# Graph network on one core: gathers that add into SBUF instead of identity matmuls, and ScalarE's and TensorE's parts of VectorE's chains issued one step later

## The chip, the core and the metric

The kernel runs on one core of a Trainium2 chip. A core has five engines with an instruction queue each, served in order: TensorE (PE, with its weight loads PEld), VectorE (DVE), ScalarE (ACT), GpSimd (POOL) and SyncE (SP). SP, ACT and POOL also issue DMAs. The metric is device microseconds (us) of one execution, from the first to the last instruction with what lies around it.

## The reference

There are 6250 nodes with 64 features and 200,000 directed edges, sorted by destination. Two graph layers follow one another, each with a residual and a layer norm around it.

```python
def layer0(v, src, dst):                       # gated attention, one head
    z = v @ Wa
    e = leaky_relu(concat([pre_w * z[src], z[dst]]) @ att_w)
    alpha = segment_softmax(e, dst)
    h = segment_sum(alpha * z[src], dst)
    pw = pre_w * v[src]
    max_feat, mean_feat = segment_max(pw @ Wg, dst), segment_mean(pw, dst)
    return sigmoid(concat([v, max_feat, mean_feat]) @ gate_w) * h

def layer1(x, edges, src, dst):                # 3 layers, 8 heads of 8
    edge_attr = relu(ln(edges) @ eW1 + eb1) @ eW2 + eb2
    for l in range(3):
        h = ln(x)
        q = h[dst] @ Wq
        k = h[src] @ Wkn + edge_attr @ Wke
        val = h[src] @ Wvn + edge_attr @ Wve
        alpha = segment_softmax((q * k).sum(-1) / sqrt(8), dst)
        agg = segment_sum(val * alpha, dst)
        gate = sigmoid(agg @ Wih + h @ Whh)
        x = x + (agg + gate * (h @ Wself - agg)) @ Wout
        x = x + relu(ln(x) @ mW1 + mb1) @ mW2 + mb2
    return ln(x)
x = ln(x + layer0(x)); x = ln(x + layer1(x))   # biases left out above
```

What matters here is the sum in `k` and `val`: a node row, looked up by the edge's source, plus a term made from the edge's own features. A table row of 128 floats holds a node's `h @ Wkn` and `h @ Wvn` side by side.

## The kernel before

**Tiling.** The nodes are sorted by degree and cut into 49 blocks (NB) of 128, one node per partition. A block's edges lie in slots along the free dimension: slot k of all 128 nodes is one column. `ORDER` runs block 1, block 48 (LB, which has 106 real nodes), block 0, then the others by falling degree.

**Edge stage** (L573 to L1004). 52 iterations (`NB + 3`), each with up to four blocks at different ages: `bs[0]` gets its lists and `masks`; `bs[1]` normalises its edge features (`even`) and sorts its slots (`select`); `bs[2]` does layer 0's attention (`absorb`) and begins the edge network; `bs[3]` ends it (`features`, half 1). `select` gives 16 of a node's slots (NW) to windows, which are later looked up by TensorE with one-hot matrices, and the rest (`LCAPS`, 14 to 40 per block, 1142 in all) to gathers.

The order is written out by hand. Each iteration has 8 steps. VectorE's work is in Python generators, which yield the cost of the piece just issued; at each step the loop takes pieces from the job that is furthest behind its weight (25 for `absorb`, 26 for the chain of `even`, `masks` and `select`) until the step's share is done (L981). A piece issues its ScalarE and TensorE instructions where they stand, such as `f_sq` (L697), `s_tg` (L752), the exponential (L896), the tanh (L934), and in `prepare` the transpose (L548), ScalarE's `fht`, the table's matmul (L559) and the copies of `p_kv` (L562, L563, L567), between which VectorE makes `p_rest` and the last part of `p_kv` (L566, L569). Around the pieces stand `aim` (VectorE's `f_mv`, L812), `order` (TensorE's `f_tr`, L825, and ScalarE's `f_xt`), and the edge network (L862, L865, L844, L848). SP issues the stores of `xd`, `x1`, `ht` and of the one-hot matrices `oh_d` (L792), and the loads `f_xs` (L805). POOL gathers layer 0's rows (L679) and stores finished table rows of a block (`place_rows`, L537).

**Three layers** (L1034 to L1282). At a layer's start ScalarE issues seven loads of the table's bf16 parts (`ftb`, L1040). Then 53 iterations take a block each. For a block, `todo` lists one window part of 16 slots and one to three gathered parts of up to 20 slots (CL). `gather` takes the next part of the whole layer as soon as one of four buffers `g1` comes free, and issues one indirect DMA per slot: 128 rows of 512 bytes from the table (L1067). `sums` adds up to 8 slots in a PSUM tile `b_pk`: TensorE first writes the edge terms (L1089), then adds for a window part the one-hot products (L1101), or for a gathered part the gathered rows by a matmul with the identity:

```python
if g is not None:
    nc.tensor.matmul(pk[:, h, :c, :], ident, g[:, u0 - k0 + h : u0 - k0 + n : 2, :], start=False, stop=True)
    continue
```

ScalarE copies the sums to `b_k` and `b_v` (L1105, L1108). VectorE multiplies with the queries (`scores`, L1112, L1113), and one iteration later makes the softmax (`soft`) and the weighted sum (`values`, L1130, L1131). The steps `turned`, `gate`, `update`, `updated`, `turned2`, `hidden`, `close` and `prepare` turn that into the node's new row, over the block's next three iterations, between the next blocks' groups of sums. SP loads edge terms (`eal`, L1051), one-hot matrices (`ohl`, L1057) and node tiles (L1073, L1075). At the end of an iteration POOL stores finished table rows for the next layer (L537), or in the last layer the output (L1221). A layer's first gather waits for all table stores of the one before.

Of the kernel before, what the change touches and what calls it, by code (L numbers as in the profile page):

```python
# [16 lines left out]
P = 128  # L17
D = 64
H = 8
# [54 lines left out]
CL = 20  # L74
# [347 lines left out]
def passes(ctx, tc, ins, out, meta_d, t0_d, own_d, ident, row_f, ones, norm_c, st_i, id_i, off, end, has, hash_, rdeg,  # L422
# [118 lines left out]
    def prepare(wk, mps, w, b, xb, i):  # L541

        tab, hd = tabs[i], ht_d[i]
        hn = wk.tile([P, D], F32, name="p_hn")
        norm(wk, hn, xb)
        yield
        pt = mps.tile([D, P], F32, name="p_pm")
        nc.tensor.transpose(pt, hn, ident)  # L548
        ht = hts[turn[0] % 3]
        turn[0] += 1  # L550
        nc.scalar.activation(ht[:D, :], pt, AF.Identity, bias=w["nrm"][:, 1:2], scale=w["nrm"][:, 0:1])

        n = P if b < LB else LN
        nc.sync.dma_start(hd[b][:, :n], ht[:, :n])
        if b == 0:
            nc.sync.dma_start(hd[LB][:, LN:P], ht[:, :SPARE])
        yield
        pm = mps.tile([P, W1], F32, name="p_pm")
        nc.tensor.matmul(pm, ht, w["wc"][:, D : 3 * D], start=True, stop=True)  # L559
        kv = wk.tile([P, WT], F32, name="p_kv", bufs=3)  # L560
        part = kv[:, W1:].bitcast(BF).rearrange("p (k d) -> p k d", k=3)
        nc.scalar.copy(kv[:, :W1], pm)  # L562
        nc.scalar.copy(part[:, 0], kv[:, :W1])  # L563
        yield
        rest = wk.tile([P, W1], F32, name="p_rest")
        nc.vector.tensor_tensor(rest, kv[:, :W1], part[:, 0], ALU.subtract)  # L566
        nc.scalar.copy(part[:, 1], rest)  # L567
        yield
# [5 lines left out]
    with tc.tile_pool(name="e1", bufs=1) as wp, tc.tile_pool(name="e_g", bufs=4) as gp, \  # L574
# [51 lines left out]
        def meet(b):  # L626
# [5 lines left out]
            ow = mp.tile([P, FO], F32, name="ow")  # L632
# [51 lines left out]
        def even(b):  # L684
# [8 lines left out]
            sqs = []  # L693
            for k0 in range(0, c, 12):
                k1 = min(k0 + 12, c)
                sq = wk.tile([P, 12, D], F32, name="f_sq")
                nc.scalar.activation(sq[:, : k1 - k0], xe[:, k0:k1], AF.Square)  # L697
                sqs.append((k0, k1, sq))
                if len(sqs) == 2:
                    yield 2.0  # L700
                    for k0, k1, sq in sqs:
                        nc.vector.tensor_reduce(sm[:, 1, k0:k1], sq[:, : k1 - k0], AX.X, ALU.add)
                    sqs = []
            if sqs:
                yield 1.5
            for k0, k1, sq in sqs:
                nc.vector.tensor_reduce(sm[:, 1, k0:k1], sq[:, : k1 - k0], AX.X, ALU.add)
# [6 lines left out]
            yield 4.5  # L714

        def select(b):
# [35 lines left out]
            nc.scalar.copy(tg[:, :c], v)  # L752
            yield 1.6

            pt = mps.tile([P, 4 * P], F32, name="p_pm")
            for h in range(2):
                nc.tensor.matmul(pt[h * D : (h + 1) * D, :D], tg, ident[:, slice(h, P, 2)], start=True, stop=True)
            m["tt"] = tt = wk.tile([P, D], F32, name="s_tt")
            nc.scalar.copy(tt, pt[:, :D])
# [21 lines left out]
            for w0 in range(0, NW, 4):  # L781
# [4 lines left out]
                bc = wk.tile([P, 4, P], F16, name="s_bc")  # L786
                nc.scalar.copy(bc, pb)
                yield 0.2
# [84 lines left out]
        def absorb(b):  # L873
# [18 lines left out]
            acc = wk.tile([P, 2 * D + 3], F32, name="a_acc")  # L892
# [3 lines left out]
            nc.scalar.activation(ex, e, AF.Exp, bias=o3[:, 0:1], accum_out=o3[:, 1:2])  # L896
            nc.vector.scalar_tensor_tensor(sc[:, 1, :], sc[:, 1, :], 1.0, vm, op0=ALU.mult, op1=ALU.mult,
                                           accum_out=o3[:, 2:3])
            yield 1.4
            for i, (k0, k1, g) in enumerate(m["g"]):  # L900
# [6 lines left out]
            for i, o, op in ((0, mx, ALU.max), (1, h, ALU.add)):  # L907
                if n == 1:
                    nc.vector.tensor_copy(o, part[:, 0, i, :])
                for j in range(1, n):  # L910
                    nc.vector.tensor_tensor(o, part[:, 0, i, :] if j == 1 else o, part[:, j, i, :], op)
            o4 = wk.tile([P, 5], F32, name="a_o4")
# [21 lines left out]
            nc.scalar.activation(o4[:, 2:3], o4[:, 2:3], AF.Tanh, bias=ow[:, D + 1 : D + 2], scale=0.5)  # L934
# [10 lines left out]
            for _ in prepare(wk, mps, nxt, b, xb, 0):  # L945
                yield 1.5
# [1028 lines left out]
```

## Time and profile before

| what | value |
|---|---|
| median of the 3 runs | 8554.21 us (8543.06 to 8555.53) |
| profiled execution | 8539.47 us |
| its span, first to last instruction | 8537.4 us |
| mean granted TensorE clock | 0.789 |
| busy in the span | PE 6224.1, PEld 4258.2, DVE 6013.9, ACT 2476.6, POOL 5161.1 us |
| before the edge stage | 0 to 110 us |
| edge stage | 110 to 3625 us |
| layers 0, 1, 2, each from its first gather | from 3625, 5261 and 6899 us; the last ends at 8537 us |
| DMA, read from and written to HBM | 899.50 and 236.89 MB |

A row of the groups gives line, engine, operation, output and inputs by the program's names, shapes and count; then busy time and mean ns of one; then the engine's idle time just before these and what ended most of it. A row of the waits gives who waited for whom, total us, times and the longest. A row of the timeline gives start, duration, engine, line, operation and, in brackets, the idle time before and its releaser; "issue" means that the trace shows nothing that was waited for. A row of the DMA queues gives packets, MB and the share of the time of 16 DMA engines.

### The profile page before, as it was taken

The page shows a single profiled execution, that of the slowest core. Times are in us where ns is not written, and L with a number is a line of the kernel's source. Part 1 is how long each engine was busy: PE and PEld are TensorE (multiplying, and loading weights), DVE is VectorE, ACT ScalarE, POOL GpSimd, SP SyncE. Part 2 cuts the span into 40 slices and gives each one's busy share as a digit, 9 for nine tenths or more (in the row PEclk, how much of TensorE's full clock was granted, in tenths as well). Part 3 has the DMA queues.
Part 4 walks back from the last instruction along what each step waited for, and adds up shares of the span by engine and source line. Part 5 has one row for each costly group of instructions (what it writes and reads, how often), then busy time and mean ns, then how long its engine had stood idle before and what let it go on. Part 6 is the DMA issues. An engine that isn't in the chain of part 4 may idle for free. (4 is left out here: it accounts for less than half of the span.)

```text
span 8537.4 us, 150270 instructions
## 1 busy us (share of the span) xinstructions
PE 6224.1 (73%) x58044; PEld 4258.2 (50%) x58044; DVE 6013.9 (70%) x13393; ACT 2476.6 (29%) x5234; POOL 5161.1 (60%) x5439
## 2 busy tenths in 40 slices
PE   3555556666656666768888886888888868888976
PEld 2222222333333333356666664666666656667765
DVE  6867778778777777647677664666676656777866
ACT  1333333333333333412222221222222212222221
POOL 4555545555444444277777773777777557777772
PEclk6767777777677676788888887888888878888887
DMA  5445444445444444366566664555566555556653
GB/s 120 130 113 131 120 118 130 127 130 134 116 117 112 112 119 124 90 171 157 145 157 155 154 150 118 147 142 149 154 155 153 134 138 134 144 146 151 159 138 77
DMA packets 965722, 1146.65 MB, mean 134 GB/s; under 512 B 665161, under 2 KB 713110, under 8 KB 957962
## 3 DMA queue, kind: packets, MB, share of 16 engines
q1 hardware_dynamic: 504569, 642.88, 24.1%
q0 software_dynamic: 180144, 412.30, 24.0%
q10 hardware_dynamic: 280288, 81.76, 4.4%
q8 instruction: 465, 7.62, 0.4%
q14 instruction: 256, 2.09, 0.1%
HBM read 899.50 MB, written 236.89 MB: 133 GB/s over the span
## 5 line engine op out<-in xcount | busy, mean ns | idle before, releaser
L1067 POOL DMA_INDIRECT g<-tab,fidx x3426 | 3275.1, 956 | 1103.5 <-issue 1009.0
L679 POOL DMA_INDIRECT g<-ft_d,si x1596 | 1527.7, 957 | 1625.1 <-DVE wx L663 1026.5
L1101 PE MATMUL b_pk<-ftb,ohl 128*128 128x128 bf16 x21609 | 1375.8, 229 | 19.4 <-DMA ftb<-tab 19.4
L1101 PEld LDWEIGHTS <-ohl 128*128 128x128 bf16 x21609 | 1325.0, 104 | 65.5 <-issue 41.4
L1112 DVE TENSOR_TENSOR b_k<-b_k,b_qe 128x1024 f32<-128x1024 f32 (+11 forms) x402 | 446.3, 1110 | 1102.9 <-ACT b_k L1105 870.3
L1093 PE MATMUL b_pk<-g,fident 128*128 128x384 f32 (+3 forms) x2172 | 1028.8, 601 | 219.9 <-DMA g<-tab,fidx 180.5
L844 PE MATMUL f_pe<-f_hid,fw 128*64 128x448 f32 (+3 forms) x2320 | 710.7, 700 | 595.1 <-ACT ea L848 594.9
L1105 ACT COPY b_k<-b_pk 128x512 f32<-128x512 f32 (+2 forms) x753 | 404.7, 537 | 2257.9 <-PE b_pk L1101 1252.3
L1089 PE MATMUL b_pk<-fwkv,eal 64*128 64x128 f32 x11556 | 1037.8, 317 | 0.0
L825 PE MATMUL f_tr<-f_mv,f_xs 128*64 128x40 f32 (+11 forms) x12544 | 603.0, 269 | 510.5 <-ACT f_xt L829 291.9
L825 PEld LDWEIGHTS f_tr<-f_mv,f_xs 128*64 128x64 f32 x12544 | 571.2, 183 | 740.3 <-issue 348.1
L1089 PEld LDWEIGHTS b_pk<-fwkv,eal 64*128 64x128 f32 x11556 | 860.2, 215 | 100.8 <-issue 27.8
L862 PE MATMUL f_ph<-f_xt,fw 64*128 64x448 f32 (+3 forms) x2320 | 723.1, 723 | 38.1 <-ACT f_xt L829 35.0
L1093 PEld LDWEIGHTS b_pk<-g,fident 128*128 128x128 f32 x2172 | 420.4, 216 | 517.1 <-issue 317.6
L1131 DVE TENSOR_REDUCE b_ag<-b_v 128x64 f32<-128x2624 f32 (+18 forms) x147 | 660.9, 4496 | 5.1
L844 PEld LDWEIGHTS f_pe<-f_hid,fw 128*64 128x64 f32 x2320 | 143.2, 168 | 1013.3 <-ACT ea L848 760.5
L865 ACT ACTIVATE f_hid<-f_ph,fb 128x896 f32<-128x896 f32 (+3 forms) x580 | 557.0, 976 | 268.9 <-PE f_ph L862 197.1
L1113 DVE TENSOR_REDUCE b_al<-b_k 128x128 f32<-128x1024 f32 (+11 forms) x402 | 446.7, 1111 | 13.8
L1105 ACT COPY b_v<-b_pk 128x512 f32<-128x512 f32 (+2 forms) x753 | 410.4, 545 | 0.0
L1130 DVE TENSOR_TENSOR b_v<-b_v,b_qe 128x2624 f32<-128x2624 f32 (+18 forms) x147 | 406.0, 2762 | 0.0
L862 PEld LDWEIGHTS f_ph<-f_xt,fw 64*128 64x128 f32 x2320 | 235.1, 238 | 292.9 <-ACT f_xt L829 147.5
L812 DVE TENSOR_TENSOR f_mv<-s_tt,e_fac 128x608 f32<-128x608 f32 (+11 forms) x392 | 313.9, 810 | 90.7 <-PE f_tr L825 52.8
(360 smaller groups left out, 7721.0 us busy)
## 6 DMA issues: line engine op xcount, KB each, us to landing
ohl<-oh_d SPq DMA_DIRECT2D x588, 384.0 KB
eal<-ea_d SPq DMA_DIRECT2D x174, 512.0 KB
oh_d<-s_oh SPq DMA_DIRECT2D x196, 384.0 KB
g<-tab,fidx POOLq DMA_INDIRECT x3426
eal<-ea_d SPq DMA_DIRECT2D x93, 384.0 KB
eal<-ea_d SPq DMA_DIRECT2D x66, 448.0 KB
ea_d<-ea ACTq DMA_DIRECT2D x130, 224.0 KB
g<-ft_d,si POOLq DMA_INDIRECT x1596
```

The costliest lines, as they stand in the source:

```text
L679: nc.gpsimd.indirect_dma_start(out=g[:, k - k0, :], out_offset=None, in_=t0_d[:], in_offset=bass.IndirectOffsetOnAxis(ap=got[b]["si"][:, k ...
L825: nc.tensor.matmul(pv[r * D : (r + 1) * D, j], xss[(4 * ORDER.index(b) + 4 * j0 // D) % 4][:, (j0 + j) % (D // 4), :], mv[:, j, :, r::2], ...
L844: nc.tensor.matmul(pe[h * D : (h + 1) * D, :w], w2[:, s, :], hid[s][:, h, :w], start=(s == 0), stop=(s == 1))
L862: nc.tensor.matmul(ph[:, h, :w], w1[r, s * P : (s + 1) * P], xf[r, e0 * D : e1 * D], start=True, stop=True)
L865: nc.scalar.activation(hid[s][:, :, :w], ph[:, :, :w], AF.Relu, bias=b1[:, s : s + 1])
L1067: nc.gpsimd.indirect_dma_start(out=g[:, k - k0, :], out_offset=None, in_=tab.rearrange("n (k d) -> (n k) d", d=D), in_offset=bass.Indirect ...
L1089: nc.tensor.matmul(pk[:, j % 2, j // 2, :], ea[r, e, :], w["wkv"][r], start=(j < 2), stop=False)
L1093: nc.tensor.matmul(pk[:, h, :c, :], ident, g[:, u0 - k0 + h : u0 - k0 + n : 2, :], start=False, stop=True)
L1101: nc.tensor.matmul(pk[:, h, j, :], o, tbh[:, cl + NW * u, i, :], start=False, stop=(j == c - 1 and u == us[-1] and i == 2))
L1105: nc.scalar.copy(to.rearrange("p (j h) d -> p h j d", h=2), pk[:, :, : n // 2, d0 : d0 + D])
L1113: nc.vector.tensor_reduce(m["al"][:, k0:k1], k.rearrange("p k (h d) -> p k h d", h=H), AX.X, ALU.add)
L1131: nc.vector.tensor_reduce(a, vv.rearrange("p k d -> p d k"), AX.X, ALU.add)
```

## The change

*Layers.* The identity matmuls are gone. `left(b)` makes the edge terms of a block's gathered parts with TensorE, ScalarE copies them (keys and values in one copy) to a tile `g1`, and the gathers then add the table rows to what lies there (`compute_op=ALU.add`). `left` for block i+1 is issued in iteration i, ahead of block i's window sums. Parts have up to 16 slots instead of 20 (96 per layer instead of 84), and there are seven `g1` buffers. Queries and weights are multiplied in place in `g1`, and `values` sums part by part. The window part has its own tile `b_kw`. The node steps run one iteration later (54 passes in place of 53), `gate` is split, and `prepare`'s ScalarE and TensorE parts are held until `then`.

*Edge stage.* A generator may yield a function: the ScalarE and TensorE instructions of a piece. The loop keeps it in `soon`, leaves that job alone for the rest of the step, and calls it in the next step; in the last step, when all jobs are held, it calls them at once and goes on. `absorb` is cut in two jobs: up to its partial sums (weight 18), and the rest with `prepare` in the next iteration (weight 6); `masks` is a job of its own (2.6), and `even` with `select` has 24.

The diff, its core (indentation cut by eight; the lines taken out are mostly those of the functions above):

```diff
--- before.py
+++ after.py
...
+CL = 16
 JB = 8
...
+def turned():
+    pt = mps.tile([D, P], F32, name="p_pm")
+    nc.tensor.transpose(pt, hn, ident)
+    nc.scalar.activation(ht[:D, :], pt, AF.Identity, bias=w["nrm"][:, 1:2], scale=w["nrm"][:, 0:1])
+    nc.sync.dma_start(hd[b][:, :n], ht[:, :n])
+    if b == 0:
+        nc.sync.dma_start(hd[LB][:, LN:P], ht[:, :SPARE])
+yield turned
+def rows():
+    pm = mps.tile([P, W1], F32, name="p_pm")
+    nc.tensor.matmul(pm, ht, w["wc"][:, D : 3 * D], start=True, stop=True)
+    nc.scalar.copy(kv[:, :W1], pm)
+    nc.scalar.copy(part[:, 0], kv[:, :W1])
+yield rows
...
+def second():
+    nc.scalar.copy(part[:, 1], rest)
+yield second
...
 nc.vector.tensor_tensor(part[:, 2], rest, part[:, 1], ALU.subtract)
 late.append((tab, b, kv))
...
+    sq = w1p.tile([P, c, D], F32, name="f_sq")
+    def squares():
+        for k0 in range(0, c, 13):
+            k1 = min(k0 + 13, c)
+            nc.scalar.activation(sq[:, k0:k1], xe[:, k0:k1], AF.Square)
+    yield 2.3
+    yield squares
...
+    def turned():
+        nc.scalar.copy(tg[:, :c], v)
+        pt = mps.tile([P, 4 * P], F32, name="p_pm")
+        for h in range(2):
+            nc.tensor.matmul(pt[h * D : (h + 1) * D, :D], tg, ident[:, slice(h, P, 2)], start=True, stop=True)
+        m["tt"] = tt = wk.tile([P, D], F32, name="s_tt")
+        nc.scalar.copy(tt, pt[:, :D])
...
+    bcs = []
+    def spread():
+        w0 = 4 * len(bcs)
...
+        bcs.append(wk.tile([P, 4, P], F16, name="s_bc", bufs=3))
+        nc.scalar.copy(bcs[-1], pb)
+    def both():
+        turned(), spread()
+    yield both
+    for w0 in range(0, NW, 4):
+        if w0 // 4 == len(bcs):
+            yield lambda: (spread(), spread() if len(bcs) < NW // 4 else None)
+        bc = bcs[w0 // 4]
...
+    def exps():
+        nc.scalar.activation(ex, e, AF.Exp, bias=o3[:, 0:1], accum_out=o3[:, 1:2])
...
     yield 1.4
+    yield exps
...
+    yield "rest"
...
+    def gates():
+        nc.scalar.activation(o4[:, 2:3], o4[:, 2:3], AF.Tanh, bias=ow[:, D + 1 : D + 2], scale=0.5)
...
     yield 2.0
+    yield gates
...
-    for _ in prepare(wk, mps, nxt, b, xb, 0):
-        yield 1.5
+    yield from prepare(wk, mps, nxt, b, xb, 0)
...
+    if bs[3] is not None:
+        jobs.append([ends.pop(0), 0.0, 6.0])
     if bs[2] is not None:
-        jobs.append([absorb(bs[2]), 0.0, 25.0])
-    second = ([even(bs[1])] if bs[1] is not None else []) + ([masks(bs[0])] if bs[0] is not None else []) \
-        + ([select(bs[1])] if bs[1] is not None else [])
-    if second:
-        jobs.append([chain(*second), 0.0, 26.0])
-    total, done = sum(j[2] for j in jobs), 0.0
+        t = absorb(bs[2])
+        jobs.append([t, 0.0, 18.0])
+        ends.append(t)
+    if bs[0] is not None:
+        jobs.append([masks(bs[0]), 0.0, 2.6])
+    if bs[1] is not None:
+        jobs.append([chain(even(bs[1]), select(bs[1])), 0.0, 24.0])
+    total, done, soon = sum(j[2] for j in jobs), 0.0, []
...
     for s in range(STEPS):
...
+        for f in soon:
+            f()
+        soon, free_jobs = [], list(jobs)
         while jobs and (done < total * (s + 1) / STEPS or s == STEPS - 1):
-            j = min(jobs, key=lambda j: j[1] / j[2])
-            w = next(j[0], None)
-            if w is None:
+            if not free_jobs:
+                if s < STEPS - 1:
+                    break
+                for f in soon:
+                    f()
+                soon, free_jobs = [], list(jobs)
+            j = min(free_jobs, key=lambda j: j[1] / j[2])
+            w = next(j[0], "rest")
+            if w == "rest":
                 done += j[2] - j[1]
...
+                free_jobs.remove(j)
+            elif callable(w):
+                soon.append(w)
+                free_jobs.remove(j)
...
-    with tc.tile_pool(name="l1", bufs=1) as fp, tc.tile_pool(name="l_g", bufs=4) as gp, \
+    with tc.tile_pool(name="l1", bufs=1) as fp, tc.tile_pool(name="l_g", bufs=7) as gp, \
...
+    todo = {b: [(b, NW + k0, NW + k1) for k0, k1 in cuts(LCAPS[b], b == ORDER[-1], CL)] for b in ORDER}
+    loads = list(todo[ORDER[0]])
+    for i, b in enumerate(ORDER):
+        loads += (todo[ORDER[i + 1]] if i + 1 < NB else []) + [(b, 0, NW)]
+    ohq = [(b, w0) for b in ORDER for w0 in range(0, NW, 4)]
+    eas, ohs = {}, {}
...
-    def gather():
-        if gathers:
-            b, k0, k1 = t = gathers.pop(0)
-            g = gs[t] = gp.tile([P, CL, W1], F32, name="g1")
-            for k in range(k0, k1):
-                f = LFIRST[b] + k - NW
-                nc.gpsimd.indirect_dma_start(
-                    out=g[:, k - k0, :], out_offset=None, in_=tab.rearrange("n (k d) -> (n k) d", d=D),
-                    in_offset=bass.IndirectOffsetOnAxis(ap=idx[:, f : f + 1], axis=0))
+    def gather(b, k0, k1, g):
+        for k in range(k0, k1):
+            f = LFIRST[b] + k - NW
+            nc.gpsimd.indirect_dma_start(
+                out=g[:, k - k0, :], out_offset=None, in_=tab.rearrange("n (k d) -> (n k) d", d=D),
+                in_offset=bass.IndirectOffsetOnAxis(ap=idx[:, f : f + 1], axis=0), compute_op=ALU.add)
...
+        ms[b] = dict(hv=hv, xb=xb, xv=xv, parts=[])
+    def sums(ea, to, k0, u0, u1, oh=None):
+        n = u1 - u0
...
-            if g is not None:
-                nc.tensor.matmul(pk[:, h, :c, :], ident, g[:, u0 - k0 + h : u0 - k0 + n : 2, :], start=False, stop=True)
-                continue
+            nc.tensor.matmul(pk[:, j % 2, j // 2, :], ea[r, e, :], w["wkv"][r], start=(j < 2),
+                             stop=(oh is None and j >= n - 2))
+        for h in range(2 if oh is not None else 0):
+            for j in range(n // 2):
...
+                    o = oh[:, unit(cl % 4, u) if u < 3 else 12, :]
...
+                                         stop=(j == n // 2 - 1 and u == us[-1] and i == 2))
+        to = to[:, u0 - k0 : u1 - k0, :]
+        if n % 2 == 0:
+            nc.scalar.copy(to.rearrange("p (j h) d -> p h j d", h=2), pk[:, :, : n // 2, :])
+            return
+        for h in range(min(2, n)):
+            nc.scalar.copy(to[:, slice(h, n, 2), :], pk[:, h, : (n + 1 - h) // 2, :])
+    def left(b):
+        for t in todo[b]:
+            k0, k1 = t[1:]
+            ea, g = eas.pop(t), gp.tile([P, CL, W1], F32, name="g1")
+            n = -(-(k1 - k0) // 8)
+            n = 2 * -(-(k1 - k0) // (2 * n))
+            for u in range(k0, k1, n):
+                sums(ea, g, k0, u, min(u + n, k1))
+            load()
+            gather(*t, g)
+            ms[b]["parts"].append((k0, k1, g))
+    def scores(m, k0, k1, g):
+        k = g[:, : k1 - k0, :D]
...
+        ps = wk.tile([P, 4, D], F32, name="b_ps")
+        for i, (k0, k1, g) in enumerate(m["parts"]):
+            vv = g[:, : k1 - k0, D:]
+            vh = vv.rearrange("p k (h d) -> p k h d", h=H)
+            nc.vector.tensor_tensor(vh, vh, ex[:, k0:k1].unsqueeze(3).to_broadcast([P, k1 - k0, H, HD]), ALU.mult)
+            nc.vector.tensor_reduce(ps[:, i], vv.rearrange("p k d -> p d k"), AX.X, ALU.add)
+        for i in range(1, len(m["parts"])):
+            nc.vector.tensor_add(a, ps[:, 0] if i == 1 else a, ps[:, i])
...
+        m["next"] = iter(())
...
+            m["then"] = next(m["next"])
...
+    def then(b, m):
+        if m.get("then"):
+            m["then"]()
...
+        m["then"] = next(m["next"], None)
...
+    for _ in range(4):
...
+    for _ in range(5):
+        load_oh()
+    begin(ORDER[0])
+    left(ORDER[0])
+    for i in range(NB + 5):
+        b, b1, b2, b3, b4 = [ORDER[i - k] if 0 <= i - k < NB else None for k in range(5)]
...
+        do(b3, updated)
+        do(b1, values)
+        do(b4, then)
+        m = ms[b] if b is not None else None
+        if i + 1 < NB:
+            begin(ORDER[i + 1])
+        if m:
+            c = SL[b]
...
+        if i + 1 < NB:
+            left(ORDER[i + 1])
+        do(b4, more)
+        do(b2, turned)
+        steps = [lambda: (do(b3, turned2), do(b2, gate, gated)), lambda: do(b3, hidden), lambda: do(b3, close, then),
+                 lambda: (do(b3, more, then), do(b2, update))]
+        if m:
+            kw = wk.tile([P, NW, W1], F32, name="b_kw")
+            ea = eas.pop((b, 0, NW))
+        for w0 in range(0, NW, 4):
+            if m:
+                sums(ea, kw, 0, w0, w0 + 4, ohs.pop((b, w0)))
...
+            steps[w0 // 4]()
+        if m:
+            load()
+            m["parts"].append((0, NW, kw))
+            for t in m["parts"][::-1]:
+                scores(m, *t)
+        do(b3, more)
...
```

## The prediction

> **What bounds the kernel now.** The sum is made against the profiled execution, 8539.47 us (span 8537.4 and 2.1 around it), 14.7 us under the median of the runs shown, 8554.21.
>
> I read busy time by stage first (columns: busy us with instruction counts of PE, weight loads, DVE, ACT, POOL; then granted clock, DMA share, GB/s). I cut it where the first gather of a layer is issued, and at the last.
>
> ```profile
> 110.00:3625.00 3515.00, 2104.76 (x18295) 1051.62 (x18295) 2651.73 (x6539) 1267.73 (x2053) 1722.10 (x1797) 0.71 0.46 121
> 3625.00:5137.00 1512.00, 1270.01 (x12480) 987.13 (x12477) 990.16 (x1905) 389.01 (x1035) 1134.05 (x1184) 0.87 0.61 155
> 5137.00:5261.00 124.00, 85.23 (x749) 65.47 (x747) 71.28 (x169) 27.66 (x75) 7.16 (x8) 0.76 0.17 46
> ```
>
> The edge stage (row 1) saturates nothing; DVE leads with 75%. In layer 0 (row 2) PE shows 84% and POOL 75%, so PE looks like the bound. The page's groups and POOL's timeline correct that:
>
> ```profile
> L1067 POOL DMA_INDIRECT g<-tab,fidx x3426 | 3275.1, 956 | 1103.5 <-issue 1009.0
> L1093 PE MATMUL b_pk<-g,fident 128*128 128x384 f32 (+3 forms) x2172 | 1028.8, 601 | 219.9 <-DMA g<-tab,fidx 180.5
> ```
> ```profile
> 5135.81 0.95 POOL L1067 DMA_INDIRECT g<-tab,fidx  x1 [0.30 <-issue]
> ...
> 5248.24 0.97 POOL L537 DMA_INDIRECT tab<-p_kv,id_i  x1 [10.52 <-DVE p_kv L569]
> 5257.43 0.97 POOL L537 DMA_INDIRECT tab<-p_kv,id_i  x1 [8.22 <-DVE p_kv L569]
> 5260.65 0.99 POOL L1067 DMA_INDIRECT g<-tab,fidx  x1 [2.25 <-issue]
> 5261.95 0.97 POOL L1067 DMA_INDIRECT g<-tab,fidx  x1 [0.30 <-issue]
> ```
>
> Each gather is followed by 0.30 us in which POOL waits for nothing: a gather costs 1.257 us. A layer has 1142 of them (3426/3) and some 44 table stores at 1.28 us inside the stream: 1435 + 56 = 1491 of 1512 us. **The layers are bound by POOL's issue rate**; PE waits for gathers (180.5 us), while POOL waits for L1093 only 54 us in all. The other part of a layer is its turn: from the last gather at 5135.81 to the next layer's first at 5260.65 POOL is nearly empty for 124.8 us.
>
> In the edge stage I read DVE's waits:
>
> ```profile
> DVE p_kv L569 <- ACT p_kv L567: 194.4, 43, 8.2
> DVE s_oh L791 <- DMA oh_d<-s_oh: 169.2, 81, 13.4
> DVE p_rest L566 <- ACT p_kv L563: 112.8, 41, 5.0
> DVE s_oh L791 <- ACT s_bc L787: 86.0, 70, 4.5
> ```
>
> These are round trips: DVE needs ACT's answer at once, while ACT stands in order behind other work.
>
> [...]
>
> **The change, part by part.**
>
> *Identity sums gone.* 1028.8 us of PE (L1093), none of it on the bound: worth nothing by itself in the stream. The b_k and b_v copies become one of twice the width; ACT is at 26% there.
>
> *Gathers after the sums.* A gather now waits for PE's edge terms and ScalarE's copy. Queued behind it on POOL are all later gathers and stores; DVE's scores wait for those. Cover: block i+1's gathers need values of block i-2 (seven buffers, two per block), and POOL then still holds blocks i-1 and i, some 23 gathers each, 2 x 29 = 58 us. The chain to be hidden (scores 5, softmax 2, values 8, gate 3, sums and copies 5) is 23 us. So I charge nothing; without that cover it would be about 20 us per block, 2900 us in all.
>
> *Price of an adding gather.* Not in this trace. Below: no reason excludes 0, [...]. The near bound: the store of the block with 106 rows beside its 128-row neighbours:
>
> ```profile
> 3848.62 0.99 POOL L537 DMA_INDIRECT tab<-p_kv,id_i  x1 [0.31 <-issue]
> 3886.65 1.57 POOL L537 DMA_INDIRECT tab<-p_kv,id_i  x1 [0.30 <-issue]
> 3924.96 0.99 POOL L537 DMA_INDIRECT tab<-p_kv,id_i  x1 [0.30 <-issue]
> ```
>
> [...] I take half, +0.05 us, [...]: 3426 x 0.05 = **+171 us**, between 0 and +343. [...]
>
> *Transfer engines.* In 3700 to 5100 us:
>
> ```profile
> q1 hardware_dynamic: 68556, 134.64, 30.1%
> q0 software_dynamic: 36281, 76.59, 30.0%
> ```
>
> A gather occupies 0.30 x 1.257 = 0.38 us of all 16 engines, 47 ns per row on its engine; everything else 0.39 us. [...] I charge nothing.
>
> *Turn of the layers.* Seven buffers and lighter PE passes mean that when the last gather is issued nothing else is behind. Of the last block there remain scores 3, softmax 2, values 8 and, as now from its finished sum (5235.6) to its table store (5257.4), 22; with the neighbour's steps between and the copies that come a step later, 45 us. Then the store lands (3), and ScalarE issues seven table loads (L1040, 16.5 us in layer 0) ahead of the copies that the first gather needs, and those copies 2. Together 67 for 125, twice: -116. Last layer: 129 becomes about 55, -74. First layer: the same loads delay its first gather, +15. Streams: 3 x (1491 + 10) for 4535, -32. Sum -207; I take **-200**.
>
> *Edge stage: parts a step later.* PE and ScalarE parts are held back and issued after DVE's pieces of the step before, so ACT no longer stands waiting (s_tg 400.6, f_sq 384.3 us) in front of feature work, and DVE finds the answers ready. Waits that go: p_kv 194.4, p_rest 112.8 + 8.1, a_o 27.6, f_mv and g behind the exponential 21.5 + 15.9: 380. Those of s_oh stay (86 from ACT, 169 from its store): the select chain adds up to about 25 units against a budget of 24, so its spreads fall into the last step, where they are flushed at once. DVE's own work hardly changes: one sum of squares for three, the rest as before. What is late next: PE (60% busy, f_tr before f_mv, 52.8 us) and the flush; I take 20 off: **-360**. The held DMAs are ht_d stores on SP, ahead of the f_xs loads; PE waits 130.5 us for those now, and the node part with its store moves an iteration later and its x1 store early in it, so I expect no more. POOL's table store comes a block later, covered, POOL being at 49%. Range: -100 (flushes eat it) to -490 (s_oh's ACT waits go too, and some of its store's).
>
> *The rest, together.* Gate, turned and prepare steps come later in a block, and the value sums are made per part with a few adds (about 1 us of DVE per block). Both lie in slack: DVE has 35% in the stream (990 of 1512), PE 38% once L1093's 343 us per layer are gone. SP loads the same edge terms and selection matrices in another order, four and five ahead. I cost these at nothing; without the slack, the 1 us is 147 us in all.
>
> **Sum:** 8539.5 - 200 - 360 + 171 = 8150; on the scale of the median, +15: **8165 us**. Own range of this case: 8539.5 - 200 - 490 = 7850 to 8539.5 - 150 - 250 + 343 = 8480, and with the median's 15 at the upper end 8495.
>
> **Rivals.**
> 1. *The transfer engines become the bound: slower.* Place: the gather stream. It binds from 108 ns per row ((1.257 - 0.39)/8), 2.3 times today's; it makes the kernel slower from 560/3426 = 0.163 us per gather, 129 ns per row. At three times (141 ns): 1.13 + 0.39 = 1.52, +0.263 us, +901: 8539.5 - 560 + 901 = 8880; at four times 10,160. For it: [...] engines 61% busy. [...] Chance 0.22.
> 2. *Issue in proportion to descriptors:* +0.478 x 3426 = 1638: 9617. Against: the 106-row store; 0.07.
> 3. *The deferral frees little:* the jobs stop at each held part, and DVE waits in the last step instead; edge gain 60: 8450. For it: four held parts per chain in eight steps. 0.16.
> 4. *The adding gathers wait on one another* (same tile, counted as written), so the change doesn't overlap them: [...]. Against: today's gathers into one tile don't wait. 0.03.
>
> **How the numbers follow.** The main case has 0.52. Faster by over 0.2% (about what a measurement of this kernel can tell from no change): 0.52 + 0.12 of the deferral rival = 0.64. Within: 0.04 of that and 0.01 of rival 1 = 0.05. Slower: 0.21 + 0.07 + 0.03 = 0.31. The range runs from 7850 (0.02 below) to 9300, which leaves out 0.07 of rival 1, rival 2 and rival 4: 0.19 together.
>
> **What would show it.** Right: the gather's duration near 1.0 us with 0.30 us issue gaps and few waits in the stream, layer turns of some 70 us, DVE's p_kv and p_rest waits near zero, an edge stage near 3155 us. Wrong: gathers with long gaps released by DMA and a DMA share near 1.0 (rival 1); a duration near 1.4 us (rival 2); new DVE waits at L765 to L791 or p_kv (rival 3); POOL waiting for the ScalarE copy block after block (cover too small).

## The result, and the profile after

The changed kernel takes **10188.02 us**, median of four runs (10185.46 to 10188.47), where the kernel before took 8548.63, also of four: ratio 1.1918, 95% interval 1.1897 to 1.1938. The forecast was 8165 us and faster; the time lies outside its range. Three runs (e9_oh, e10_old_add, e11_oh) fell in a disturbed stretch in which the kernel before itself took 12885 us; nothing is read from their times, and the same kernels ran again as e13_oh, e12_old_add and e14_oh.

The windows of the changed kernel, cut as before (edge stage, stream of layer 0, turn; busy us with counts of PE, weight loads, DVE, ACT, POOL, then clock, DMA share, GB/s):

```profile
110.00:3403.00 3293.00, 1924.13 (x18339) 985.77 (x18340) 2655.88 (x6462) 1287.08 (x2048) 1712.90 (x1797) 0.74 0.48 131
3403.00:5590.00 2187.00, 1094.89 (x12372) 969.35 (x12369) 1062.77 (x2255) 395.68 (x873) 1825.48 (x1185) 0.72 0.54 106
5590.00:5673.00 83.00, 25.32 (x114) 18.74 (x113) 31.53 (x105) 10.59 (x31) 6.21 (x7) 0.54 0.33 97
```

The edge stage is 222 us shorter (3293 for 3515) and the turn 41 us (83 for 124), but each stream grew from 1512 to 2187 us, while PE's busy share of it fell from 84% to 50% and the DMA share from 0.61 to 0.54. POOL's busy time rose by far the most, from 1134 to 1825 us. Its group says why, and its timeline shows the end of the stream and the turn:

```profile
L1112 POOL DMA_INDIRECT g<-tab,fidx x3426 | 5346.9, 1561 | 1120.6 <-issue 991.9
```
```profile
5586.95 1.56 POOL L1112 DMA_INDIRECT g<-tab,fidx  x1 [0.31 <-issue]
5588.81 1.56 POOL L1112 DMA_INDIRECT g<-tab,fidx  x1 [0.30 <-issue]
...
5642.06 0.96 POOL L537 DMA_INDIRECT tab<-p_kv,id_i  x1 [8.95 <-DVE p_kv L578]
5673.08 1.59 POOL L1112 DMA_INDIRECT g<-tab,fidx  x1 [30.07 <-ACT g L1147]
```

The same 3426 gathers take 1561 ns each for 956, the 0.30 us of issue between them is unchanged, and nothing else stands between them: 1.862 us a gather for 1.257. The edge stage's plain gathers stay at 952 ns. 1142 x 1.862 + 44 x 1.3 = 2184 us is the stream. The queue of the gathers, over the same 3700 to 5100 us as before:

```profile
q0 software_dynamic: 106752, 52.78, 30.8%
```

That is 494 bytes a packet: the rows of 512 bytes now go singly. In the whole execution this queue sent 563,856 packets for 180,144 with the same 412.30 MB, 112 more per gather, so 128 for 16. The queue's share is about what it was (30.0%), but with fewer gathers in it: counted as in the prediction, a gather occupies 0.308 x 1.862 = 0.57 us of all 16 engines, 72 ns of an engine's time per row, 1.5 times the 47 of before.

In the edge stage VectorE's longest waits are now, beside those at s_oh (167 us for the store, 73 for ScalarE):

```profile
DVE f_mv L831 <- PE f_tr L844: 86.3, 15, 8.7
...
DVE f_sm L711 <- ACT f_sq L707: 70.1, 18, 6.6
DVE p_kv L578 <- ACT p_kv L575: 22.1, 3, 11.6
...
DVE p_rest L572 <- ACT p_kv L568: 13.6, 4, 4.5
```

The waits at p_kv and p_rest are nearly gone (194 and 121 us before); those at f_tr (53 before) and f_sq (2 before) grew.

### The profile page after: what moved, and what is told of

It is laid out like the page before. It is cut to its first block, busy times and chain, and to the rows that moved or that the text cites. A ratio compares the mean times of both kernels' runs of the same rounds, so it can differ in the third digit from the quotient of the medians.

```text
span 10185.9 us, 146541 instructions
## 1 busy us (share of the span) xinstructions
PE 5235.0 (51%) x55872; PEld 3895.8 (38%) x55872; DVE 6124.8 (60%) x14231; ACT 2470.4 (24%) x4618; POOL 7227.2 (71%) x5439
## 3 DMA queue, kind: packets, MB, share of 16 engines
q0 software_dynamic: 563856, 412.30, 26.3%
## 5 line engine op out<-in xcount | busy, mean ns | idle before, releaser
L1112 POOL DMA_INDIRECT g<-tab,fidx x3426 | 5346.9, 1561 | 1120.6 <-issue 991.9
L1134 PE MATMUL b_pk<-fwkv,eal 64*128 64x128 f32 x11556 | 1161.5, 344 | 3162.1 <-ACT g L1147 3103.8
L1134 PEld LDWEIGHTS b_pk<-fwkv,eal 64*128 64x128 f32 x11556 | 966.2, 239 | 3274.6 <-ACT g L1147 3142.3
L1143 PE MATMUL b_pk<-ftb,ohl 128*128 128x128 bf16 x21609 | 1503.9, 236 | 0.0
L1167 DVE TENSOR_TENSOR g<-g,b_qe 128x768 f32<-128x768 f32 (+8 forms) x291 | 271.6, 933 | 1941.2 <-DMA tab<-p_kv,id_i 723.6
L1147 ACT COPY b_kw<-b_pk 128x512 f32<-128x512 f32 x588 | 344.6, 586 | 1644.9 <-PE b_pk L1143 1630.8
L1167 DVE TENSOR_TENSOR b_kw<-b_kw,b_qe 128x1024 f32<-128x1024 f32 x147 | 179.1, 1219 | 667.7 <-ACT b_kw L1147 667.7
L1147 ACT COPY g<-b_pk 128x768 f32<-128x768 f32 (+2 forms) x480 | 385.6, 833 | 263.6 <-PE b_pk L1134 205.1
L1188 DVE TENSOR_REDUCE b_ps<-g 128x64 f32<-128x768 f32 (+9 forms) x291 | 420.1, 1444 | 10.0
L848 ACT ACTIVATE f_xt<-f_tr,feg 128x304 f32<-128x304 f32 (+11 forms) x392 | 240.9, 615 | 574.5 <-PE f_tr L844 552.8
```

Of the source, the lines that this page charges most:

```text
L1112: nc.gpsimd.indirect_dma_start(out=g[:, k - k0, :], out_offset=None, in_=tab.rearrange("n (k d) -> (n k) d", d=D), in_offset=bass.Indirect ...
L1134: nc.tensor.matmul(pk[:, j % 2, j // 2, :], ea[r, e, :], w["wkv"][r], start=(j < 2), stop=(oh is None and j >= n - 2))
L1143: nc.tensor.matmul(pk[:, h, j, :], o, tbh[:, cl + NW * u, i, :], start=False, stop=(j == n // 2 - 1 and u == us[-1] and i == 2))
L1147: nc.scalar.copy(to.rearrange("p (j h) d -> p h j d", h=2), pk[:, :, : n // 2, :])
L1167: nc.vector.tensor_tensor(k, k, m["q"].unsqueeze(1).to_broadcast([P, k1 - k0, D]), ALU.mult)
L1188: nc.vector.tensor_reduce(ps[:, i], vv.rearrange("p k d -> p d k"), AX.X, ALU.add)
```

## The experiments

**The price alone, taken out (e1_plain).** The changed kernel, its gathers plain again:

```diff
-                        in_offset=bass.IndirectOffsetOnAxis(ap=idx[:, f : f + 1], axis=0), compute_op=ALU.add)
+                        in_offset=bass.IndirectOffsetOnAxis(ap=idx[:, f : f + 1], axis=0))
```

> The changed kernel with its gathers issued without the addition: the rows overwrite the edge terms, so the terms of the gathered slots are left out of keys and values; order, buffers, waits and copies stay. Theory 'price': what the changed kernel lost is POOL's time for an adding gather, 1.561 us where a plain one takes 0.956; then the gathers go back to 0.95 us with 0.30 us between them, each stream from 2187 to about 2187 - 1142 x 0.605 = 1496 us, and the time is 10188 - 3426 x 0.605 = 8115 us, 40 either way. Rival 'order': the gathers' waiting for edge terms and copies, and the later node steps, cost part of it; then POOL shows waits for ScalarE's copy and the time stays above 8250, in proportion to that part (8550 if it is half of what isn't price).

Measured: 8450.62 us, ratio to the kernel before 0.9893 (0.9878 to 0.9908). The gather is back at 956 ns, but only 1738 of the 2073 us came back, and POOL now waits:

```profile
POOL g L1112 <- ACT g L1147: 293.0, 56, 29.8
```

```profile
L1112 POOL DMA_INDIRECT g<-tab,fidx x3426 | 3275.2, 956 | 1361.4 <-issue 931.3
```

So the rival 'order' holds too, for 335 us: some 240 of them in the streams (1595, 1593 and 1544 us, where 2187 less 1142 x 0.605 is 1496), the rest in the turns and at the end. From about 4480 us on, where a block has 22 gathers or fewer, blocks come every 30.4 to 33.6 us though POOL needs less. One such round in the timeline of all engines:

```profile
4850.54 0.59 ACT L1147 COPY b_kw<-b_pk 128x512 f32<-128x512 f32 x1 [3.89 <-PE b_pk L1143]
...
4857.78 0.44 DVE L1176 TENSOR_TENSOR b_al<-b_al,b_md 128x272 f32<-128x272 f32 x1
4858.26 0.40 ACT L1177 ACTIVATE b_qe<-b_al 128x272 f32<-128x272 f32 x1 [6.64 <-DVE b_al L1176]
...
4858.78 1.28 ACT L1147 COPY g<-b_pk 128x768 f32<-128x768 f32 x2
...
4859.84 0.97 POOL L1112 DMA_INDIRECT g<-tab,fidx  x1 [6.71 <-ACT g L1147]
```

Read it backwards: the gather waits for ScalarE's copy of its edge terms; that copy stands in ScalarE's queue behind the exponential of the block before (6.64 us of waiting); the exponential waits for the scores, and these for the copy of the block's last window sum, 8 us earlier. The window sums of the next block come after that on TensorE, with the node steps between them. So each block's gathers wait for a chain that starts in the block before; this closed chain is called the ring below. In the changed kernel POOL takes some 35 us over such a block (18 x 1.862 + 1.3), and the ring lies under it.

**The ring, half undone (e4_early, e7_after_early).** The next block's edge terms, copies and gathers are issued ahead of the exponential:

```diff
+                if i + 1 < NB:
+                    begin(ORDER[i + 1])
+                    left(ORDER[i + 1])
                 do(b1, soft)
...
-                if i + 1 < NB:
-                    begin(ORDER[i + 1])
...
-                if i + 1 < NB:
-                    left(ORDER[i + 1])
```

With plain gathers:

> As e1_plain (plain gathers that overwrite the edge terms of the gathered slots), but each iteration issues the next block's edge-term sums, copies and gathers ahead of the softmax of the block before, not behind it. In e1_plain the streams took 1614 us for 1494 us of POOL's own, and the blocks of the second half came every 30.5 us. Theory 'loop': ScalarE's copy that releases the gathers stands behind the exponential, which waits for the scores, which wait for the last window sum, which is issued behind the copy: a ring of 30 us per block that the adding gathers (35 us per block) had covered. Then POOL's waits for the copies (293 us) fall under 60 in the streams, a stream takes about 1500 us, and the time is 8450 - 3 x 113 = 8111 us, 40 either way. Rival 'tensor engine': the ring is PE's own order of windows and node steps (67% busy, each step a round trip), which stays; then the blocks still come every 30 us and the time stays within 60 of 8450.

Measured: 8312.18 us, 0.9715 (0.9684 to 0.9747): 138 us of the 335. The streams take 1541, 1536 and 1505 us, 150 less in all, while the rest of the kernel takes some 18 longer. The blocks at the end of the first stream still come every 29 us:

```profile
POOL g L1112 <- ACT g L1147: 142.5, 36, 29.9
```

Neither theory had it whole. The exponential was a part of the ring; what is left agrees with the rival's picture of TensorE's order of windows and node steps, which no run took apart further. With adding gathers:

> The changed kernel with only its order altered as in e4_early; the gathers add. Theory 'loop': the ring of 30 us per block lies under the 35 us of POOL there, so the streams stay at 2187 us and the time at 10188 us, 30 either way. Rival: part of the 10188 is the ring's; then the time falls by 50 us or more.

Measured: 10187.64 us, 1.191 (1.1861 to 1.1958). In the changed kernel the ring costs nothing.

**The price in the old order (e12_old_add).** The kernel before, with `compute_op=ALU.add` on its gathers and four fixed g1 tiles set to zero at the beginning:

> The kernel of e10_old_add again: the kernel before with gathers that add to what its four buffers hold (the gathered rows in the sums are wrong by that). Theory 'price': 1.56 us and 0.30 us of issue per gather in the old order too (the disturbed call showed 1.559), a stream of 2183 us for 1512, and 8549 + 3 x 671 = 10562 us, 40 either way. Rival: the identity sums, which this kernel keeps, wait for gathers that land later, and lengthen the turns of the layers; then the time is 10650 or more.

Measured: 10462.49 us, 1.2244 (1.2221 to 1.2266), 100 us under the expectation. The gather takes 1560 ns here as well, and each stream 2185 us, so the price doesn't depend on the order:

```profile
L1071 POOL DMA_INDIRECT g<-tab,fidx x3426 | 5343.4, 1560 | 1065.4 <-issue 897.5
```

What was not expected: the turns shrank, from 124 to 90 and 92 us, and the end after the last gather from 129 to 80, although the layers' order is the old one; less 15 us by which the first gather comes later, that is most of the missing 100. A slower stream leaves TensorE less to catch up with when it ends: in the first turn it does 494 matmuls here and did 749 before. Most of the shorter turns of the changed kernel is this and not its order: with plain gathers (e1_plain) its turns are 114 and 105 us.

**The price by itself (m1_price, m2_rows).** Sixteen gathers of each kind, one after the other, nothing beside them; m2_rows has other numbers of rows.

```python
g.indirect_dma_start(out=t["add64"][:64, k, :], out_offset=None, in_=tab, in_offset=off(k, 64), compute_op=ALU.add)
```

> No part of the computation: sixteen transfers each of fifteen kinds, one after the other on POOL's queue, with VectorE and TensorE idle: plain and adding indirect gathers of 128 rows of 256, 512 and 1024 bytes, adding ones of 112, 64 and 32 rows, plain ones of 120, 106, 96 and 64 rows, and direct transfers of the same shape, plain and adding. Theory 'rows': an adding gather issues every row by itself, [...]; then adding 512-byte rows take 1.56 us here too, 256 and 1024 bytes the same within 0.1, 64 rows near 1.16 [...], 32 rows near 0.96, and plain 106 rows [...] are as dear as the store of 106 rows, 1.4 to 1.6. Rival 'bytes': 256 bytes 1.26, 1024 bytes 2.2. Rival 'fixed': 64 and 32 rows stay above 1.45. Rival 'neighbours': the price comes from what runs beside it in the layers; then an adding gather takes 1.0 to 1.1 us here.

Measured: plain, 128 rows of 256, 512 and 1024 bytes 947, 955 and 950 ns. Adding, 128 rows of 512 bytes (L42), 64 rows (L46), 256 bytes (L58), 1024 bytes (L62); and plain with 106 rows (L52):

```profile
L52 POOL DMA_INDIRECT plain<-in_x_dram,idx x16 | 24.8, 1552 | 4.9 <-issue 4.9
L42 POOL DMA_INDIRECT add<-in_x_dram,idx x16 | 24.7, 1543 | 4.9 <-issue 4.9
L58 POOL DMA_INDIRECT add<-in_x_dram,idx x16 | 24.7, 1542 | 4.9 <-issue 4.9
L62 POOL DMA_INDIRECT add1k<-in_x_dram,idx x16 | 24.7, 1541 | 4.9 <-issue 4.9
...
L46 POOL DMA_INDIRECT add<-in_x_dram,idx x16 | 22.8, 1422 | 4.9 <-issue 4.9
```

The layers' price is there without neighbours; bytes don't count; and with half the rows it falls by only 0.12 us, to 1.34 at 32 rows. 'Rows', 'bytes' and 'neighbours' fall; 'fixed' comes nearest, though it asked for more than 1.45 us at 64 and 32 rows. Nor does the price hang on the lookup: of the transfers of the same shape without indices, sixteen plain ones (L66) occupy POOL for 8.7 us and sixteen adding ones (L68) for 14.4, so 0.54 and 0.90 us each. That a plain gather of 106 rows costs the same looked like one cause for both:

> No part of the computation: sixteen indirect gathers of 512-byte rows each with 128, 127, 126, 124, 122, 120, 116, 112, 108, 104, 100 and 72 rows, plain, and with 128, 120, 106 and 16 rows, adding. The changed kernel's gathers sent 112 more packets each (128 single rows for 16 packets of eight), and a plain gather of 106 rows cost as much as an adding one, where 96, 112 and 120 didn't. Theory 'eights': a gather whose rows can't be sent in groups is issued row by row, whatever the reason, and that is the dear way; then 120, 112, 104 and 72 take 0.90 to 0.98 us, 127, 126 and 122 take 1.4 to 1.65, 124, 116, 108 and 100 lie with one or the other, and adding takes 1.27 us + 2.1 ns per row: 1.30 at 16 rows, 1.49 at 106. Rival 'two prices': the 106 rows are a case of their own [...]; then the other counts that aren't multiples of eight lie between 0.95 and 1.5, with no jump.

Measured: here plain with 128 (L39), 127 (L41), 124 (L45) and 122 rows (L47), and adding with 106 (L67):

```profile
L39 POOL DMA_INDIRECT plain<-in_x_dram,idx x16 | 15.4, 959 | 33.1 <-DVE idx L20 28.6 <-issue 4.6
L45 POOL DMA_INDIRECT plain<-in_x_dram,idx x16 | 20.5, 1279 | 4.9 <-issue 4.9
L47 POOL DMA_INDIRECT plain<-in_x_dram,idx x16 | 26.6, 1661 | 4.9 <-issue 4.9
L41 POOL DMA_INDIRECT plain<-in_x_dram,idx x16 | 40.7, 2545 | 4.9 <-issue 4.9
L67 POOL DMA_INDIRECT add<-in_x_dram,idx x16 | 43.6, 2722 | 4.9 <-issue 4.9
```

'Eights' falls: 126 rows take 0.980 us and 100 rows 0.993. What the times of these two runs do follow is the rows divided by the largest number up to 16 that divides them, called the quotient here: 128 are 16 x 8, quotient 8, 126 14 x 9, 124 4 x 31, 106 2 x 53, 122 2 x 61, 127 1 x 127. All plain ones fit 0.85 us + 13.3 ns per unit of the quotient, within 0.03 us (31: 1.26, measured 1.279; 53: 1.55, measured 1.552 in m1_price; 61: 1.66, measured 1.661; 127: 2.54, measured 2.545). This is a fit to the times; what the quotient stands for, no trace shows. The adding ones are another line: 16 x 1 rows 1.309, 16 x 2 1.340, 16 x 4 1.422, 16 x 8 1.544, 15 x 8 1.595, 2 x 53 2.722: 1.28 us + 26 to 39 ns per unit of the quotient, 33 ns at 128 rows. **Of the 0.59 us that the addition costs at 128 rows, 0.43 is fixed and 8 x 20 ns = 0.16 goes with the quotient**, by these two lines. Why 0.43 us more is fixed, no run shows.

**The edge stage alone (e2_edge).** The changed edge stage with the layers of the kernel before, `prepare`'s held parts called in place there:

> The changed kernel's edge stage with the layers of the kernel before (identity sums, plain gathers, parts of 20, four buffers; the held parts of a node's table rows are issued in place there). Theory 'price': the edge stage keeps its 245 us and the layers return to 1512 us and turns of 125 us, so 8549 - 245 = 8304 us, 30 either way. Rival: the end of the edge stage only looks shorter because the first layer's start took over some of it; then the first gather comes later than 3403 us by as much, and the time is 8400 or more.

Measured: 8297.46 us, 0.9711 (0.9698 to 0.9724). The first gather starts at 3384 us for 3626; 242 us are the edge stage's, as 'price' expects, for 360 in the forecast. (With the new layers the first gather comes 19 us later, at 3403; the forecast charged 15 for that.) Where the other 118 us went, the following edits of e2_edge ask.

The transpose held one step more (e3_turn):

```diff
-            yield from prepare(wk, mps, nxt, b, xb, 0)
+            t = prepare(wk, mps, nxt, b, xb, 0)
+            turned = next(t)
+            yield lambda: None
+            yield turned
+            yield from t
```

> As e2_edge, but in the edge stage the held transpose of a block's normalised rows is held one step more. In the changed kernel TensorE stands 394 us in 39 places at that transpose, because it is issued at a step's start, before VectorE has made the rows. Theory 'standing': these stands make feature work late and so cause VectorE's new waits (f_tr 86, f_sq 70 us); then the stands fall under 100 us and the time is 60 to 120 us below that of e2_edge. Rival 'loads': the features' own loads are late (TensorE waits 228 us for f_xs) and set those waits; then the time is that of e2_edge within 20 us.

Measured: 8311.00 us, 0.9733 (0.9720 to 0.9746). TensorE's stands at the transpose fell from 390 to 151 us, but VectorE's waits at f_tr and f_sq stayed (84 to 80 and 68 to 71 us), and nothing was gained. 'Standing' falls.

The squares in place, by undoing that part of the diff (e6_sq):

> As e2_edge (8297 us), but the squares of the edge features are not held: ScalarE gets them in place, in chunks of 12 slots, as in the kernel before. Theory 'held squares': the hold of this part brings nothing, since VectorE now waits 68 us for the squares at f_sm where it waited 2 before; then that wait goes and the time is 20 to 60 us lower. Rival: in place the squares stand in front of other work on ScalarE, as before, and the waits move to f_mv, p_kv or s_oh; then the time is the same within 20 us or higher.

Measured: 8306.16 us, 0.9710 (0.9683 to 0.9737), no difference. VectorE's wait for the squares went from 68 to 11 us, and the old ones came back:

```profile
DVE p_kv L578 <- ACT p_kv L575: 100.6, 11, 12.3
DVE a_o L971 <- ACT a_o L964: 62.2, 19, 19.5
```

The feature loads issued at the beginning of a step, ahead of that step's stores on SP (e5_xs):

```diff
+                n = 4 * (i - 2) + s // 2 + 2
+                due = s % 2 == 1 and 0 <= n < 4 * NB
+                if due and "xd" in got[ORDER[n // 4]]:
+                    bring(n)
+                    due = False
                 half = 2 * s // STEPS
...
```

> As e2_edge (8297 us), but SP issues the loads of the sorted edge features (f_xs) at the beginning of a step, ahead of that step's stores, wherever the stored features are already there. Theory 'loads': SP's stores stand in order in front of the loads and wait for VectorE (740 us at the xd store, 737 at the one-hot store), which makes TensorE wait 237 us for f_xs and VectorE for TensorE (f_mv 73) and ScalarE (f_sq 68); then TensorE's wait for f_xs falls under 100 us and the time is 60 to 130 us lower. Rival 'rate': the loads are late because 30,000 packets of 256 bytes a time take long to move, wherever they are issued; then the wait stays above 180 us and the time within 20 us of 8297.

Measured: 8273.29 us, 0.9673 (0.9646 to 0.9699), 24 us better. TensorE's wait for f_xs fell from 237 to 27 us and VectorE's for f_tr and f_sq to 5 us each, so the cause of those waits is as theory 'loads' says. (TensorE stood for another 114 us at f_tr where the trace shows no releaser. And a load of 124 KB is some 500 packets of 256 bytes, not the 30,000 of rival 'rate'.) But the gain isn't there, because one wait took their place (158 us in e2_edge):

```profile
DVE s_oh L810 <- DMA oh_d<-s_oh: 319.8, 89, 34.0
...
DVE f_sm L711 <- ACT f_sq L707: 5.5, 2, 3.2
```

Four buffers for the one-hot matrices, with those early loads (e13_oh) and without (e14_oh). To make room, two tiles (s_m, s_li) move into the tile of the squares, and `ow` has one buffer less; what that costs by itself was not tried.

```diff
...
-            me = w1p.tile([P, NW, c], F32, name="s_m")
+            box = m["sq"].rearrange("p c d -> p (c d)")
+            me = box[:, : NW * c].rearrange("p (w c) -> p w c", w=NW)
...
-                oh = wk.tile([P, 4, 3, P], BF, name="s_oh")
+                oh = wk.tile([P, 4, 3, P], BF, name="s_oh", bufs=4)
```

> The kernel of e9_oh again (early loads, four s_oh buffers), since in that call the kernel before itself took 12885 us, with TensorE idle for 2784 us at the window sums where nothing was waited for, so that nothing can be read from it. Theory 'store': VectorE's 320 us at s_oh for the one-hot stores fall under 100, and the time is 8273 - 150 to 8273 - 230 us. Rival 'queue': SP issues the stores late behind loads that wait for TensorE; more buffers move the wait by little and the time stays above 8230.

> The kernel of e11_oh again (four s_oh buffers, loads where the changed kernel has them). Theory 'next in line': the 158 us at s_oh go, the 141 us for f_tr and f_sq stay or grow; the time is 60 to 130 us below 8297 and above that of e13_oh by 30 or more. Rival: the store's wait alone sets the stage's length; then the time is that of e13_oh within 15 us.

Measured: e13_oh **8197.17 us**, 0.9593 (0.9580 to 0.9606), e14_oh 8237.72 us, 0.9639 (0.9626 to 0.9652). The waits for the store are gone in both. e14_oh meets 'next in line', at the near end of its 60 to 130 us. e13_oh gained 76 us, between what the two theories had: f_mv waits for TensorE again, in e13_oh

```profile
DVE f_mv L832 <- PE f_tr L845: 149.2, 18, 22.5
```

In the same stage TensorE stands at f_ph for ScalarE's f_hid, 159 us for 10 in e5_xs. So no single wait held the 118 us; in these runs each wait that goes uncovers another, and the gain is a part of it. e13_oh is the fastest kernel of this study: the changed edge stage, two repairs to it, and the layers of before.

## Why the prediction was wrong

Its own sum against the profiled execution, times of the first and last gathers from POOL's timeline (us); the two columns at the right are the new order and the old one with the other kind of gather:

| term | before | predicted | after | e1_plain | e12_old_add |
|---|---|---|---|---|---|
| first gather of layer 0 | 3626 | 3281 | 3403 | 3405 | 3641 |
| streams | 1511, 1514, 1509 | 1558 each | 2187, 2190, 2188 | 1595, 1593, 1544 | 2185, 2186, 2185 |
| turns of layers | 124, 124 | 67, 67 | 83, 75 | 114, 105 | 90, 92 |
| last gather to the end | 129 | 55 | 60 | 90 | 80 |

Predicted to after: 122 + 1891 + 24 + 5 = 2042 us. **1891 of them are one term.**

*Bound of the layers, POOL's issue rate: right.* With TensorE's identity sums gone and the DMA share lower, the streams are still 1142 times duration and gap. 'Identity sums gone, worth nothing' fits too: PE busy in the stream fell from 1270 to 1095 us, and no run without the identity sums has a stream more than 5 us shorter than before.

*Price of an adding gather: the step that failed.* The forecast took the store of 106 rows, 1.57 us for 0.99, as its near bound and came to 0.10 us at most (343 us over 3426 gathers), of which it took half. How much of the 0.58 us between the stores an addition would pay again was the author's estimate, which the trace did not show. By the two lines above, the part that goes with the quotient came out at 0.16 us, for 0.10 and the 0.05 that was taken. But the step took for granted that the fixed part stays, and that grew by 0.43. Measured +0.605 x 3426 = 2073 us for 171. Nothing in the profile excluded that; the store has no addition in it and so could bound the part that goes with the rows only. The range inherited the mistake, with 0.10 us as its far end in the main case; its own upper end, 8480, is also narrower than its terms, as it takes 250 us off for the edge stage, whose range ended at 100. Rival 2, half of the plain gather's 0.956 us more, came nearest in size (1.43 us, 9617) on a wrong scale: the price is not in proportion to what is sent, as an adding gather takes 1.543 us with 128 rows and still 1.422 and 1.340 with 64 and 32 (m1_price).

*Transfer engines not the bound: right.* A row costs them 72 ns in the stream, and rival 1 needed 108. Of an adding row to a plain one the ratio is 1.5 in the layers (72 to 47 ns), but 2.3 in m1_price, where ten plain gathers take 12.5 us at a queue share of 19.3% and ten adding ones 18.45 us at 30.4%, 30 and 70 ns a row. So alone an adding row costs the engines more than twice a plain one; in the layers the ratio is smaller because the plain rows take 47 ns there for 30, and why they do was not tried. Rival 4 didn't occur either: in all 3426 gathers POOL waits 35 us for an earlier gather.

*Gathers after the sums, cover 58 us against a chain of 23: wrong, though it cost nothing.* The prediction looked at buffers coming free. The ring goes through ScalarE's order, exponential ahead of copies (e4_early), and, as far as can be argued from the trace, through TensorE's; it takes 30.5 us per block at the stream's end, and the cover is POOL's work on one block, 25 us for 20 plain gathers. With plain gathers (e1_plain) the streams are up to 94 us longer than the 1501 that the forecast had before its price, 229 in all. The slow gathers hid it.

*Turn of the layers: near in number, wrong in reason.* 157 us for the two, forecast 134. But e12_old_add gets 182 with the old order, and e1_plain 219 with the new one; by itself the new order gives back 29 of 248 us, not 114. With the slow gathers TensorE has 114 matmuls left in the first turn, with plain ones 335.

*Edge stage: mechanism right, one term mis-sized.* The waits named did go: p_kv 194 to 22, p_rest 121 to 14, a_o 28 to 3, those behind the exponential 37 to 1, 340 of 380. Those of s_oh stayed, as forecast. "What is late next ... 20 off" is the term: f_sq took 68 us, f_tr 33, smaller ones some 35 together, 136 for 20; some 50 us of other waits that the forecast had not named went as well. And "the held DMAs ... I expect no more" of TensorE's wait for f_xs was wrong: 130 before, 236 after. e5_xs ties the f_tr and f_sq waits to those loads. Why they come later in the changed kernel than before was not tried by itself.

## What to carry to other kernels

Split the price of an operation that the trace doesn't show into a part that is fixed and a part that grows, and bound each from a row that contains that part; a row without the operation says nothing of its fixed part. Where an issue rate is the bound, multiply both bounds by the count before choosing one: 0.1 us was 343, 0.6 us 2073. A wait that is taken out of a chain of engines, each of which works in order, is worth only the time until the next wait in line takes hold, here 242 of 380 us, then 24 of some 140 and 76 of 320.

## What the runs showed of the hardware that was not expected

- An indirect DMA of 127 rows holds POOL for 2.545 us, one of 128 rows 0.959; 106 adding rows take 2.722, 128 adding rows 1.544. By these numbers the block of 106 nodes would be cheaper to move as 128 rows; that wasn't tried.
- The price of a gather on POOL is the same for 256-, 512- and 1024-byte rows (947 to 955 ns plain, 1541 to 1543 adding).
- An adding transfer costs POOL more without a lookup too: 0.90 us for 0.54 (m1_price, direct transfers).
- Adding gathers send each 512-byte row as a packet of its own, 128 packets for 16. In the layers a row then takes 72 ns of a transfer engine's time, where eight rows in a packet take 47 each; with nothing beside them (m1_price) it is 70 for 30.
